# Elu from one exp and one max on products that carry a + 1, and the last layer's scores as extra columns of the eight-head layer

## The chip, the cores and the metric

The kernel runs on one core of one Trainium2 chip. The metric is the device time of one execution in microseconds (us). The engines are named as the profile does: PE (TensorE matmuls), PEld (TensorE weight loads), DVE (VectorE), ACT (ScalarE), POOL (GpSimd) and SP (SyncE, which issues most DMAs). Everything is fp32. Line numbers with an L are those of the kernel before, as its profile has them.

## The reference, cut to what matters

There are 128 independent graphs of 128 nodes with 512 features. Each passes four layers, and after each layer the input is added back and the sum is normalized over its features (`x = norm(x + layer(x))`).

- Layer 0: attention over the neighbours, scores from two dot products with `x`, output `attn @ x`.
- Layer 1: two graph attention layers. `xl = x @ W1` is 4 heads of 256, each with its own scores; the output of the four heads plus `b1` goes through an elu; then one head of 512 with `W2` and `b2`:

```python
h = jax.nn.elu(gat_layer(x, mask, W1, att_src1, att_dst1, b1, concat=True))
h = gat_layer(h, mask, W2, att_src2, att_dst2, b2, concat=False)
```

- Layer 2: 8 heads of 64, each with two score vectors, outputs concatenated.
- Layer 3: scores from `x @ W_fc.T` times the two halves of `W_attn`, attention applied to `x` itself, then an elu:

```python
h = jnp.einsum('bni,oi->bno', graph_input, W_fc)
f1 = jnp.einsum('bno,o->bn', h, a1)
f2 = jnp.einsum('bno,o->bn', h, a2)
...
h_prime = jnp.einsum('bnm,bmi->bni', attn, graph_input)
return jax.nn.elu(h_prime)
```

## The kernel before, in words

**One graph is one tile.** The 128 nodes lie on the 128 partitions. `graph(g)` (L314) lists the operations of one graph, each with its engine, an assumed cost, its inputs and its outputs; nothing is emitted there.

**A planner sets the order of every engine.** `Pipeline.plan` (L71) places the operations of one graph on the five engines, modulo a period (`PERIOD`, 24.7 before), from the assumed costs, fixed latencies (`LATENCY`), a weight on the rest of the path (`URGENCY`, 0.6) and a random shift for each operation (`SEED`, `SPREAD`: 62, 8.0). `Pipeline.run` (L124) then lays 128 copies of that plan one period apart, sorts all operations by planned time and emits them in that order. So many graphs are in flight at once, each engine runs its instructions strictly in that order, and the real times follow from the waits alone. A buffer gets a slot by its planned life; there are 8 PSUM banks. The loads and preparations of the weights are further entries with planned times of their own (`at(t, ...)`, L206).

**What one graph does:**

- Layer 0: two scores of `x` on VectorE (`score`, L493: multiply, add up, L495), `spread` (L326: transpose of a score column on VectorE, a DMA to a row in DRAM, a DMA that broadcasts it over the partitions), `attend` (L378), `mixed` (L467: one 512-column product of the attention with `x`), `resid` (L512), `norm` (L419).
- `attend` for some heads: leaky relu on ScalarE (L387), mask and row minimum on VectorE (L395), exp with its row sum on ScalarE (L404), reciprocal (L412), and with `scaled=True` a multiplication by the reciprocal on GpSimd (L414). Without it, the reader of the product multiplies. Then `turned` (L343): the attention is transposed by 32x32 blocks on VectorE (L348), written to DRAM and read back by DMA.
- `norm`: statistics on VectorE (L422, L423), the root on GpSimd (L426, L427), and the normalization on VectorE (L439), or with `on_act=True` on ScalarE (L435) with an offset from GpSimd (L432). After layer 2 it is on VectorE.
- Layer 1: `project` (L444) multiplies the transposed input with the weights in pieces of columns and copies each piece out of PSUM. `w1a` is 4 blocks of rows by 1032 columns (the 1024 of `W1` and 8 score columns), in 3 pieces of 344, evicted by ScalarE (L461). `block` (L535) makes half of the four heads' output in one bank, features on the partitions: 4 of the kernel's matmuls of 128 columns, 8 for both halves (L540). Then ScalarE makes exp(x + b1) and relu(x + b1), with `b1` as a bias for each partition, so in four pieces of 128 columns each (L549), and VectorE makes min(exp - 1, relu), the elu (L555). `w2a` is 8 blocks by 514 columns in 2 pieces of 257.
- Layer 2: `wha` is 4 blocks by 528 columns (512 and 16 score columns) in 2 pieces of 264. `heads` (L579) does 4 heads: 4 products of 64 columns (L585) and a multiplication by the reciprocals on VectorE (L590). GpSimd adds the input (L598).
- Layer 3: two scores of the normalized `x3` on VectorE (L603, L604, with the columns `wf`), attention, a `mixed` product, exp and relu on ScalarE with the reciprocal as scale (L609, L610), min(exp - 1, relu) on VectorE (L611), the input added on GpSimd (L614), norm on ScalarE, output.

**A matmul of the kernel is two MATMUL records and two LDWEIGHTS records in the profile**, so the counts of the profile are twice those of the code.

**Preparation**, mixed into the first graphs: the loads of `w1a`, `w2a`, `b2t` and of the score vectors go over GpSimd's queue, those of `wha` over SP's, that of `b1t` over ScalarE's. VectorE makes the score columns of the weights: `dot` (L263) for `w1a` (32 times) and `w2a` (16 times), `dots` (L280) for `wha` (8 pairs of a multiplication and a reduction). `columns` (L294) makes `wf` with two products (L298).

Of the kernel before, what the change touches and what calls it, by code (L numbers as in the profile page):

```python
# [16 lines left out]
P = 128  # L17
# [10 lines left out]
PERIOD = 24.7  # L28
LATENCY = {"PE": (0.0, 0.8), "DVE": (0.15, 1.4), "ACT": (0.1, 1.4), "POOL": (0.1, 1.4), "SP": (6.0, 6.0)}
URGENCY = 0.6  # L30
BANKS = 8

SEED, SPREAD = 62, 8.0
# [117 lines left out]
def tile_gat_stack(  # L151
# [48 lines left out]
    nc.vector.memset(neghalf, -0.5)  # L200

# [18 lines left out]
    def passing(t, until, n, src=None):  # L220
# [8 lines left out]
    C1, C2, C3 = HF + 2 * H1, F + 2, F + 2 * H2  # L229
# [5 lines left out]
    w1a = weights(-19, [P, KF, C1], "w1a", *(  # L235
        (lambda w, b=b: w[b::4, :, :HF], w1.rearrange("(k b a) c -> b a k c", b=4, a=32)[b])
        for b in range(4)
    ))
    a1 = [passing(-18, 90, HF, a.rearrange(flat).partition_broadcast(P)) for a in (a1_src, a1_dst)]
    b1t = weights(-18, [P, KH], "b1t", (lambda w: w, b1.rearrange("(k p) -> p k", p=P)), by=nc.scalar)  # L240
    b2t = rows(16, b2, F, "b2t")
    w2a = weights(18, [P, KH, C2], "w2a", *(
        (lambda w, k=k: w[:, k : k + 2, :F], w2[k * P : (k + 2) * P].rearrange("(k p) c -> p k c", p=P))
        for k in range(0, KH, 2)
# [3 lines left out]
    fc = passing(60, 270, F, w_fc)  # L248
# [5 lines left out]
        (lambda w, b=b, k=k: w[b::4, k, :F].rearrange("p (h o) -> p h o", h=H2),  # L254
# [3 lines left out]
    acb = [passing(240, 270, P) for _ in range(2)]  # L258
    wf = const.tile([P, 2, F], F32, name="wf")
    prod = [passing(-20, 230, F) for _ in range(2)]  # L260
    turn = [0]
# [9 lines left out]
    for k in range(KF):  # L271
        for s in range(2):
            for h in range(H1):
                c, o = slice(h * FH, (h + 1) * FH), HF + s * H1 + h
                at((31, 33, 56, 58)[k] + s + h / 4, lambda k=k, s=s, c=c, o=o: dot(w1a[:, k, c], a1[s].ap[:, c], w1a[:, k, o : o + 1]))
    for k in range(KH):
        for s in range(2):
            at(100 + 3 * k + 1.5 * s, lambda k=k, s=s: dot(w2a[:, k, :F], a2[s].ap, w2a[:, k, F + s : F + s + 1]))

    def dots(k, s):  # L280

        turn[0] ^= 1
        pr = prod[turn[0]].ap
        nc.vector.tensor_mul(pr, wha[:, k, :F], a3[s].ap)
        nc.vector.tensor_reduce(
            out=wha[:, k, F + s * H2 : F + (s + 1) * H2], in_=pr.rearrange("p (h o) -> p h o", h=H2),
            op=ALU.add, axis=AX.X,
        )

    for k in range(KF):  # L290
        for s in range(2):
            at(190 + 6 * k + 3 * s, lambda k=k, s=s: dots(k, s))

    def columns(s):  # L294
# [4 lines left out]
        nc.vector.tensor_copy(wf[:, s, :], pf)  # L299

    for s in range(2):
        at(250 + 3 * s, lambda s=s: columns(s))
# [11 lines left out]
    def graph(g):  # L314
# [63 lines left out]
        def attend(db, h0, nh, src, mask, scaled=False):  # L378
# [34 lines left out]
            if scaled:  # L413
                op("POOL", 1.3, lambda: nc.gpsimd.tensor_mul(  # L414
# [4 lines left out]
        def norm(y, on_act=False):  # L419
# [10 lines left out]
            if on_act:  # L430
                mr = small("mr", 1)
                op("POOL", 0.3, lambda: nc.gpsimd.tensor_scalar(  # L432
                    out=mr.ap, in0=mv.ap[:, 0:1], scalar1=rd.ap, scalar2=-1.0, op0=ALU.mult, op1=ALU.mult
                ), [mv, rd], [mr])
# [3 lines left out]
                return  # L438
# [5 lines left out]
        def project(xT, wa, nk, ncol, nchunk, t, evict):  # L444

            w = ncol // nchunk

            def chunk(c, ev):
                px = bank()
                cols = slice(c * w, (c + 1) * w)  # L450

                for k in range(nk):
                    op("PE", w * 4 / 2400 + 0.006, lambda k=k: nc.tensor.matmul(  # L453
                        px.ap[:, :w], lhsT=xT.ap[:, k, :], rhs=wa[:, k, cols],
                        start=(k == 0), stop=(k == nk - 1),
                    ), [xT] if k == 0 else [xT, px], [px])
                if ev == "DVE":
                    op("DVE", 0.11 + w / 960, lambda: nc.vector.tensor_copy(  # L458
                        t.ap[:, cols], px.ap[:, :w]), [px], [t])
# [196 lines left out]
```

## Time and profile before

| | before |
|---|---|
| median of 3 runs | 3200.89 us (3199.28 to 3202.06) |
| the profiled execution | 3201.2 us |
| its span, first to last instruction | 3199.3 us |
| mean granted TensorE clock | 0.983 |
| PE busy | 3073.7 us (96%), 14212 records |
| DVE busy | 3003.9 us (94%) |
| ACT busy | 2444.6 us (76%) |
| POOL busy | 1563.7 us (49%) |
| DMA queue 1 | 589.44 MB, 74.8% of 16 engines' span |

Busy time is the time in which at least one record of the engine runs. Matmuls overlap in the records, so what one costs is read from the distance of starts, not from its duration. A group of the profile is named by line, engine, operation and tiles; most work tiles share the name `w`. The profile's window "10 graphs in mid-run" is 1000 to 1236.45 us, ten times the distance at which the same work of the next graph starts; in it DVE is busy 233.48 us, ACT 190.53 and POOL 121.27.

### The profile page before, as it was taken

The numbers are of one execution on the slowest core, as the hardware profiler recorded it, in microseconds if no ns is written. First come the engines' busy times: TensorE is split into PE (matmuls) and PEld (weight loads), VectorE is DVE, ScalarE is ACT, GpSimd is POOL, SyncE is SP. The second block draws the span as 40 slices with busy tenths as digits, with TensorE's granted clock in tenths as the row PEclk, the third lists the DMA queues.
The fourth block names the chain that finished last, engine by engine and source line by source line (L and its number), as shares of the span: only waits on it lengthen the run. The fifth ranks groups of instructions, "written<-read, shape, count | busy, mean of one in ns | idle before, by whom it ended". The sixth has DMA issues, their size and how long they took to land.

```text
span 3199.3 us, 60449 instructions
## 1 busy us (share of the span) xinstructions
PE 3073.7 (96%) x14212; PEld 2378.0 (74%) x14212; DVE 3003.9 (94%) x9976; ACT 2444.6 (76%) x8961; POOL 1563.7 (49%) x2328
## 2 busy tenths in 40 slices
PE   3999999999999999999999999999999999999974
PEld 1677777777777777777777777777777777777762
DVE  5768999999999999999999999999999999999885
ACT  1567888877878788788787887878878878788864
POOL 4334545555545455555455554545555545555334
PEclk9999999999999999999999999999999999999985
DMA  4467787777878777788787777777777787778774
GB/s 149 116 154 186 190 196 196 195 197 193 199 192 198 193 198 194 196 197 197 191 199 196 193 196 195 197 196 196 194 199 193 195 196 197 197 192 196 175 167 112
DMA packets 1640373, 600.46 MB, mean 188 GB/s; under 512 B 1310464, under 2 KB 1490688, under 8 KB 1640016
## 3 DMA queue, kind: packets, MB, share of 16 engines
q1 hardware_dynamic: 1636608, 589.44, 74.8%
q0 software_dynamic: 1936, 6.62, 0.6%
q8 instruction: 115, 1.88, 0.3%
q14 instruction: 242, 1.98, 0.2%
q10 hardware_dynamic: 1472, 0.53, 0.1%
HBM read 368.91 MB, written 227.48 MB: 186 GB/s over the span
## 4 chain that ended last, share of the span: by engine, by line
PE 93%; DVE 3%; DMA 2%; POOL 1%; ACT 1%; issue 1%; SPq 0%; ACTq 0%; POOLq 0%; DVEq 0%
PE ps L453 69%; PE ps L470 10%; PE ps L540 7%; PE ps L585 6%; DMA w<-scr 1%; DVE w L495 0%; PE ps L506 0%; DMA scr<-w 0%; ACT w L404 0%; DVE w L395 0%; DVE st L422 0%; DMA w_-1_4_139<-in_L_gnn_att_dst_dram 0%; POOL rd L427 0%; DVE w L348 0%; DVE w_-1_1_94 L266 0%
## 5 line engine op out<-in xcount | busy, mean ns | idle before, releaser
L453 PE MATMUL ps<-w2a,w 128*128 128x257 f32 x4096 | 953.2, 380 | 3.1 <-DVE xl L458 3.1
L453 PE MATMUL ps<-w1a,w 128*128 128x344 f32 x3072 | 917.2, 455 | 1.9 <-ACT w L549 0.9
L453 PEld LDWEIGHTS ps<-w2a,w 128*128 128x128 f32 x4096 | 758.3, 190 | 121.1 <-DVE xl L458 3.9
L453 PEld LDWEIGHTS ps<-w1a,w 128*128 128x128 f32 x3072 | 587.4, 191 | 348.6 <-issue 41.1
L404 ACT ACTIVATE w<-w,nm 128x128 f32<-128x128 f32 x1920 | 767.3, 412 | 31.9 <-DVE nm L395 26.6
L387 ACT ACTIVATE w<-w,xl 128x128 f32<-128x128 f32 x1664 | 543.5, 447 | 265.5 <-DVE w L513 239.6
L395 DVE CUSTOM_DVE_ANT_0 w<-w,w 128x128 f32<-128x128 f32 x1920 | 666.3, 456 | 24.7 <-ACT w L387 11.6
L549 ACT ACTIVATE w<-ps,b1t 128x128 f32<-128x128 f32 x2048 | 560.6, 404 | 112.3 <-PE ps L540 112.3
L348 DVE STREAM_TRANSPOSE w<-w 128x512 f32<-128x512 f32 (+1 forms) x1024 | 544.0, 541 | 32.3 <-PE ps L540 9.1
L426 POOL TENSOR_SCALAR rd<-mv 128x1 f32<-128x1 f32 x512 | 118.5, 232 | 920.5 <-DVE mv L423 894.3
L453 PEld LDWEIGHTS ps<-wha,w 128*128 128x128 f32 x2048 | 390.4, 191 | 121.4 <-issue 36.8
L453 PE MATMUL ps<-wha,w 128*128 128x264 f32 x2048 | 480.0, 388 | 0.0
L461 ACT COPY xl<-ps 128x344 f32<-128x344 f32 (+2 forms) x640 | 277.9, 435 | 175.3 <-PE ps L453 165.8
L404 ACT ACTIVATION_READ_ACCUMULATOR w<-w,nm 128x1 f32 x1920 | 401.2, 209 | 0.0
L523 POOL TENSOR_TENSOR w<-w,b2t 128x512 f32<-128x512 f32 x128 | 165.9, 1296 | 467.5 <-DVE w L348 282.0
L585 PEld LDWEIGHTS ps<-xl,w 128*128 128x128 f32 x2048 | 295.3, 197 | 104.2 <-issue 78.9
L422 DVE BATCH_NORM_STATS2 st<-w 128x6 f32<-128x512 f32 x512 | 353.9, 691 | 11.8 <-POOL w L614 7.3
L427 POOL TENSOR_TENSOR rd<-rd,neghalf 128x1 f32<-128x1 f32 x512 | 307.4, 600 | 42.7
L470 PE MATMUL ps<-w,w 128*128 128x512 f32 x512 | 281.7, 633 | 32.5 <-DMA w<-scr 16.1
L585 PE MATMUL ps<-xl,w 128*128 128x64 f32 x2048 | 278.5, 271 | 25.4 <-DVE mv L423 9.9
L395 DVE DVE_READ_ACCUMULATOR2_ANT nm<- 128x1 f32 x1920 | 291.4, 152 | 0.0
L495 DVE CUSTOM_DVE_ANT_0 w<-w,wf 128x512 f32<-128x512 f32 x256 | 282.2, 1103 | 0.0
(74 smaller groups left out, 3913.7 us busy)
## 6 DMA issues: line engine op xcount, KB each, us to landing
scr<-w SPq DMA_DIRECT2D x640, 256.0 KB
w<-scr SPq DMA_DIRECT2D x640, 256.0 KB
w<-row SPq DMA_DIRECT2D x128, 512.0 KB
w<-in_x_dram SPq DMA_DIRECT2D x128, 256.0 KB
w<-row SPq DMA_DIRECT2D x128, 256.0 KB
out_dram<-w SPq DMA_DIRECT2D x128, 256.0 KB
w<-row SPq DMA_DIRECT2D x384, 64.0 KB
scr<-w SPq DMA_DIRECT2D x384, 64.0 KB
```

The costliest lines, as they stand in the source:

```text
L348: op("DVE", 0.12 + 0.133 * n, lambda: nc.vector.transpose(zb.ap.rearrange("p b h c -> p h b c"), src.ap.rearrange("p (h b c) -> p h b c", ...
L387: nc.scalar.activation(z.ap[:, h, :], db.ap[:, h0 + h, :], AF.Prelu, bias=src(h0 + h), alpha=SLOPE)
L395: nc.vector.tensor_tensor_reduce(out=zz.ap[:, h, :].rearrange("p (b a) -> p a b", b=4), in0=z.ap[:, h, :].rearrange("p (a b) -> p a b", b= ...
L404: nc.scalar.activation(zz.ap[:, h, :], zz.ap[:, h, :], AF.Exp, bias=nm.ap[:, h : h + 1], scale=-1.0, accum_out=rs.ap[:, h : h + 1],)
L422: op("DVE", 0.6, lambda: nc.vector.bn_stats(st.ap, y.ap), [y], [st])
L427: nc.gpsimd.tensor_tensor(out=rd.ap, in0=rd.ap, in1=neghalf, op=ALU.pow)
L453: op("PE", w * 4 / 2400 + 0.006, lambda k=k: nc.tensor.matmul(px.ap[:, :w], lhsT=xT.ap[:, k, :], rhs=wa[:, k, cols], start=(k == 0), stop= ...
L461: op("ACT", 0.16 + w / 1200, lambda: nc.scalar.copy(t.ap[:, cols], px.ap[:, :w]), [px], [t])
L470: op("PE", width * 4 / 2400, lambda: nc.tensor.matmul(pa.ap[:, :width], lhsT=pt.ap[:, 0, :], rhs=xv.ap[:, :width], start=True, stop=True), ...
L495: op("DVE", 0.75, lambda: nc.vector.tensor_tensor_reduce(out=jk.ap, in0=xv.ap, in1=wv, scale=1.0, scalar=init, op0=ALU.mult, op1=ALU.add, ...
L549: nc.scalar.activation(out.ap[:, k, :], pa.ap[:, u * P : (u + 1) * P], func, bias=b1t[:, k : k + 1])
L585: op("PE", 0.225, lambda u=u, h=h: nc.tensor.matmul(pa.ap[:, u * FO : (u + 1) * FO], lhsT=pt.ap[:, u, :], rhs=xl3.ap[:, h * FO : (h + 1) * ...
```

## The change

- **Elu.** Since elu(v) + 1 = max(v + 1, min(exp(v), 1)), the products now carry v + 1: ScalarE makes exp(p - 1) of the product p in one instruction of 512 columns, VectorE makes max(min(exp, 1), p) with p read from PSUM. So Relu falls away in both Elus. In layer 1, `b1 + 1` is added to `xl` by GpSimd (two additions of 512 columns) after the scores were taken; since the attention is now scaled to sum 1, that adds it to the products. The + 1 that remains in the hidden features is taken out by preparation: minus the column sums of `w2a` go into `b2t` (`ones_out`) and into two score shifts (`shifts`), which one small addition of VectorE puts on each graph's scores (`sc2`). In layer 3, `norm` adds the 1 to its offset, the normalization moves from VectorE to ScalarE, and the attention is scaled by GpSimd (`scaled=True`).
- **Scores of the last layer.** They are linear in the normalized sum of layer 2's output and its input. So each head of `wha` gets two more columns (its rows times `wf`, by head), 66 columns for each head, and two columns for the input's own part; `wha` is 546 columns in 2 pieces of 273. The head products give the two partial scores beside the 64 features, VectorE adds up the 8 heads (16 elements), adds the input's part, and applies mean and root (`normed`). Both `score` calls after layer 2 fall away.
- **Pieces.** `w1a` is stored by head, 258 columns each (256 and 2 scores), in 4 pieces instead of 3. `w2a` is two halves of 256 with one score column each.
- **Loads.** `w1a` comes in 16 loads (4 before), `w2a` in 8 (4 before), `b1` as a row for all partitions over GpSimd's queue.
- **Planner.** `PERIOD` 24.9, `URGENCY` 1.0, `SEED` 17, `SPREAD` 3.0, some assumed costs; so the whole order is drawn anew.

```diff
-PERIOD = 24.7
+PERIOD = 24.9
-URGENCY = 0.6
+URGENCY = 1.0
-SEED, SPREAD = 62, 8.0
+SEED, SPREAD = 17, 3.0
...
+    def ones_out(s):
+        pf = psum.tile([P, 512], F32, tag=f"ps{6 + s}", name=f"pc_{s}")
+        for k in range(KH):
+            nc.tensor.matmul(
+                pf[:, : F // 2], lhsT=minus, rhs=w2a[:, k, s, : F // 2], start=(k == 0), stop=(k == KH - 1)
+            )
+        cols = slice(s * F // 2, (s + 1) * F // 2)
+        nc.vector.tensor_add(b2t[:, cols], b2t[:, cols], pf[:, : F // 2])
...
+    def shifts():
+        pf = psum.tile([P, 512], F32, tag="ps7", name="pc_2")
+        for k in range(KH):
+            nc.tensor.matmul(pf[:, :2], lhsT=minus, rhs=w2a[:, k, :, F // 2], start=(k == 0), stop=(k == KH - 1))
+        nc.vector.tensor_copy(shift2, pf[:, :2])
...
     for k in range(KF):
         for s in range(2):
-            at(190 + 6 * k + 3 * s, lambda k=k, s=s: dots(k, s))
+            at(160 + 12 * k + 6 * s, lambda k=k, s=s: dots(k, a3[s], slice(SH + s * H2, SH + (s + 1) * H2)))
+            at(163 + 12 * k + 6 * s, lambda k=k, s=s: dots(k, wf[s], slice(FO + s, SH, CH)))
...
+        for k in range(KF):
+            pf = psum.tile([P, 512], F32, tag="ps7", name=f"pg_{k}")
+            nc.tensor.matmul(pf[:, :2], lhsT=fcp.ap[:OUT, k * P : (k + 1) * P], rhs=ac, start=True, stop=True)
+            nc.vector.tensor_copy(wha[:, k, C3 - 2 :], pf[:, :2])
...
+        for h in range(0, H1, 2):
+            op("POOL", 1.3, lambda h=h: nc.gpsimd.tensor_add(
+                xl.ap[:, h : h + 2, :FH], xl.ap[:, h : h + 2, :FH],
+                b1t[:, h * FH : (h + 2) * FH].rearrange("p (h c) -> p h c", h=2),
+            ), [xl], [xl])
...
-            op("ACT", 1.1, lambda: biased(e1, AF.Exp), [pa], [e1])
-            op("ACT", 1.1, lambda: biased(r1, AF.Relu), [pa], [r1])
-            op("DVE", 0.6, lambda: nc.vector.scalar_tensor_tensor(
-                out=half(hT), in0=half(e1), scalar=-1.0, in1=half(r1), op0=ALU.add, op1=ALU.min
-            ), [e1, r1], [hT])
+            op("ACT", 0.6, lambda: nc.scalar.activation(half(e1), pa.ap, AF.Exp, bias=minus[:, 0:1]), [pa], [e1])
+            op("DVE", 0.65, lambda: nc.vector.scalar_tensor_tensor(
+                out=half(hT), in0=half(e1), scalar=1.0, in1=pa.ap, op0=ALU.min, op1=ALU.max
+            ), [e1, pa], [hT])
...
-        norm(x3)
-        score(x3, wf[:, 1, :], 0.0, sc4, 1)
-        score(x3, wf[:, 0, :], 0.0, sc4, 0)
+        def scores():
+            nc.vector.tensor_reduce(
+                out=sc4.ap, in_=z3.ap[:, :, FO:].rearrange("p h s -> p s h"), op=ALU.add, axis=AX.X
+            )
+            nc.vector.tensor_add(sc4.ap, sc4.ap, xl3.ap[:, C3 - 2 :])
+
+        op("DVE", 0.2, scores, [z3, xl3], [sc4])
+        mv, rd = norm(x3, on_act=True, plus=1.0)
+
+        def normed():
+            nc.vector.scalar_tensor_tensor(
+                out=sc4.ap, in0=swf, scalar=mv.ap[:, 0:1], in1=sc4.ap, op0=ALU.mult, op1=ALU.add
+            )
+            nc.vector.tensor_scalar_mul(sc4.ap, sc4.ap, rd.ap)
+
+        op("DVE", 0.15, normed, [sc4, mv, rd], [sc4])
...
-        op("ACT", 0.7, lambda: nc.scalar.activation(e3.ap, pa.ap, AF.Exp, scale=ri.ap), [pa, ri], [e3])
-        op("ACT", 0.7, lambda: nc.scalar.activation(r3.ap, pa.ap, AF.Relu, scale=ri.ap), [pa, ri], [r3])
-        op("DVE", 0.6, lambda: nc.vector.scalar_tensor_tensor(
-            out=y.ap, in0=e3.ap, scalar=-1.0, in1=r3.ap, op0=ALU.add, op1=ALU.min
-        ), [e3, r3], [y])
+        op("ACT", 0.6, lambda: nc.scalar.activation(e3.ap, pa.ap, AF.Exp, bias=minus[:, 0:1]), [pa], [e3])
+        op("DVE", 0.65, lambda: nc.vector.scalar_tensor_tensor(
+            out=y.ap, in0=e3.ap, scalar=1.0, in1=pa.ap, op0=ALU.min, op1=ALU.max
+        ), [e3, pa], [y])
```

## The prediction, as put on record

> **What bounds the kernel now.** I read the page's busy shares and its chain first, then TensorE's timeline over one graph in mid-run, then stretches of the span, and last the groups of VectorE, ScalarE and GpSimd. The page's shares of busy time and of the chain that ended last:
>
> ```profile
> PE 3073.7 (96%) x14212; PEld 2378.0 (74%) x14212; DVE 3003.9 (94%) x9976; ACT 2444.6 (76%) x8961; POOL 1563.7 (49%) x2328
> ...
> PE 93%; DVE 3%; DMA 2%; POOL 1%; ACT 1%; issue 1%; SPq 0%; ACTq 0%; POOLq 0%; DVEq 0%
> ```
>
> TensorE carries 93% of the chain, but VectorE is nearly as busy, so busy shares alone don't settle it. The timeline of TensorE does (start, us, then the group; "idle before" would stand in brackets):
>
> ```profile
> 999.77 6.81 PE L453 MATMUL ps<-w1a,w 128*128 128x344 f32 x23
> 1006.43 3.20 PE L453 MATMUL ps<-w2a,w 128*128 128x257 f32 x14
> 1009.46 0.33 PE L585 MATMUL ps<-xl,w 128*128 128x64 f32 x2
> ...
> 1016.51 1.45 PE L585 MATMUL ps<-xl,w 128*128 128x64 f32 x12
> 1017.80 1.08 PE L470 MATMUL ps<-w,w 128*128 128x512 f32 x2
> 1018.71 3.72 PE L453 MATMUL ps<-wha,w 128*128 128x264 f32 x16
> 1022.27 1.02 PE L470 MATMUL ps<-w,w 128*128 128x512 f32 x2
> ```
>
> No line has an idle time: each group starts where the last ends. Start to start, a 344-column matmul record costs 6.66/23 = 289 ns, a 257-column one 3.03/14 = 217 ns, a 264-column one 3.56/16 = 222.5 ns: a slope of (289 - 222.5)/80 = 0.83 ns a column and about 2.5 ns besides. The 64-column ones cost 1.29/12 = 107 ns, far over what that slope gives; they are held by their weight loads. One graph costs 23.65 us, as the chain shows too:
>
> ```profile
> 384.87 9.97 PE ps L453 x38
> 408.52 9.97 PE ps L453 x38
> ```
>
> The stretches of the span (us, busy PE, PEld, DVE, ACT, POOL with counts, then granted clock, DMA share, GB/s):
>
> ```profile
> 0.00:100.00 100.00, 41.46 (x106) 22.65 (x107) 55.37 (x202) 19.74 (x66) 39.34 (x62) 0.92 0.52 147
> 100.00:225.00 125.00, 120.89 (x518) 89.36 (x518) 83.71 (x264) 72.81 (x268) 40.88 (x61) 0.99 0.49 126
> 225.00:3040.00 2815.00, 2815.00 (x13238) 2197.97 (x13237) 2753.75 (x9130) 2261.03 (x8327) 1419.24 (x2107) 1.00 0.79 195
> 3040.00:3187.00 147.00, 94.50 (x354) 67.79 (x353) 108.60 (x378) 87.28 (x296) 58.66 (x89) 0.72 0.62 146
> ```
>
> From 225 to 3040 us TensorE is busy for every microsecond. So span = 128 x 23.65 = 3027 us of matmuls, and 172 us of fill and drain. Summing over all matmuls the time to the next start beyond its full-clock spacing splits the 172 into 12 us before the first matmul, 67 up to 225 us, 80 from 3040 us to the last matmul, 11.5 after it, and some 2 of setup products.
>
> The groups that the change touches (name, shapes, count, then busy us, mean ns, idle before):
>
> ```profile
> L495 DVE CUSTOM_DVE_ANT_0 w<-w,wf 128x512 f32<-128x512 f32 x256 | 282.2, 1103 | 0.0
> ...
> L439 DVE TENSOR_SCALAR w<-w,mv,rd 128x512 f32<-128x512 f32 x256 | 243.2, 950 | 4.6 <-POOL rd L427 3.9 <-issue 0.6
> ...
> L523 POOL TENSOR_TENSOR w<-w,b2t 128x512 f32<-128x512 f32 x128 | 165.9, 1296 | 467.5 <-DVE w L348 282.0 <-PE ps L453 153.8 <-DMA w<-row 21.6
> ...
> L611 DVE SCALAR_TENSOR_TENSOR w<-w,w 128x512 f32<-128x512 f32 x128 | 153.5, 1199 | 0.4 <-ACT w L609 0.4
> ...
> L609 ACT ACTIVATE w<-ps,ri 128x512 f32<-128x512 f32 x128 | 85.6, 668 | 1.1 <-DVE sc L495 1.1
> ```
>
> **What the Trainium skill says.** "TensorE: Matmul & The Clock Gate", section "Back-to-back issue gap", gives columns/2.4 + 2.5 ns for a warm matmul; the trace agrees with twice the column term for each fp32 record (344 x 2/2.4 + 2.5 = 289.2). The same page, "LDWEIGHTS (loading the stationary operand)", gives columns/1.2, 107 ns for 128: that is the 107 ns of the 64-column products, so their width is free. "GPSIMD Engine Reference", "Specifications": its SBUF interfaces are shared with VectorE, against operations with two SBUF inputs or in a two-port mode. The trace agrees for L495 with wf, 676 ns in mid-run where no GpSimd work overlaps, against a mean of 1116 there, but not everywhere: L555, also with two SBUF inputs, takes 675 either way.
>
> **The change, part by part, per graph in mid-run.**
> TensorE. First layer: 24 records of 344 columns (24 x 289.2 = 6.940) become 32 of 258 (32 x 217.7 = 6.966): +0.03. Second layer: 257 columns as before: 0. Third layer: 16 of 264 become 16 of 273, 222.5 + 9 x 0.83 = 230.0: +0.12. Head products 64 to 66 columns: 0, hidden under the weight load (uncovered, 16 x 1.7 = 0.03). The rest is unchanged. Sum +0.148 us, so 23.79 us a graph, and 128 x 0.148 = +18.9 us, all on the path.
>
> VectorE. Off: two scores L495 (2 x 1.12, 2 x 0.08 for their read-outs), one of two L439 (1.01), the last Elu reading PSUM and no longer two SBUF tiles (1.28 to the 0.72 of L513): -3.97. On: the first Elu from PSUM, 2 x 0.05; a 16-element reduce, three tiny operations and the sum of second-layer scores, 5 x about 0.13 (L412's 119 ns to L423's 179): +0.75. So 23.35 (ten graphs in mid-run, 233.5 us busy) falls by 3.2 to about 20.1, before more GpSimd overlap. Overlap now adds about 3.7 us (each group's mean less its mean clear of GpSimd), of which some 1.7 stays exposed; with GpSimd busier by a third that grows by 0.6. 20.7 is under 23.79: nothing on the path.
>
> ScalarE, 19.05: 16 biased activations, union 4.38, become 2 of 512 columns at 0.67 (-3.05); one Relu off (-0.67); third norm on (+0.81); one more eviction (+0.1 to +0.5). About 16.4: hidden. GpSimd, 12.1: b1 adds 2 x 1.29, the last layer's scaling 0.36 (between L414's 1.04 for four heads and 0.23), mr and its +1, 0.53 + 0.23: about 15.8. The b1 adds follow the evictions; in the new order a graph's mixing products come two graphs after its first layer's, so some 45 us hide them. If POOL were late, they would hold those products and w2a behind them. SP's issues stay equal in number.
>
> Fill. (a) w1a takes 16 loads for 4 on GpSimd's queue, at about 0.55 us each, w2a 8 for 4, b1t moves there with 512 KB more: +10 us of issue ahead of graph 0's and 1's masks. Most is hidden: GpSimd idles 4.9 and 7.7 us there. But 16 products of minus and w2a (32 records, 7 to 14 us by clock) now stand before graph 0's first mixing product at 33.5 us, and the b1t add waits on its load at VectorE. I take +3 (0 to +9). (b) The shift products and last columns: 24 records x 0.112 = 2.7, and four round trips with VectorE at about 0.5: +4.7 (2 to 7). (c) In the new order w2a of the first three or four graphs follows directly on that graph's mixing products; in the old one 9 w2a products, a mixing product and w1a lie between. So TensorE waits for exp, Elu and release, about 2 us a graph: +7 (2 to 10), until later layers fill the gap. The 16 dot pairs of 1.37 us (8 before) double to 22 us of VectorE in the same rounds, and take part of that cover; no more added. Sum about +14.
>
> Drain. In the new order a final mixing product comes 3 graphs behind its heads, not 4, so one product fewer follows the last heads; the last graph's path loses a norm and two scores (about 2.5), a Relu (0.67), and gains POOL's scaling and two tiny steps (0.9). With VectorE lighter in the thinned rounds: -7 (0 to -16).
>
> Against the profiled execution (3201.2, span 3199.3): 3201.2 + 18.9 + 14 - 7 = 3227; the runs' median is 0.3 lower, 3200.9. I predict 3227.
>
> **The rivals.** *The drain repays it (not slower).* In the drained rounds TensorE waits for loads of transposed attention, behind VectorE's queue:
>
> ```profile
> 3080.00:3100.00 20.00, 13.16 (x44) 9.62 (x43) 16.05 (x56) 12.17 (x43) 8.58 (x13) 0.66 0.72 179
> 3100.00:3120.00 20.00, 13.32 (x44) 9.37 (x43) 12.62 (x48) 11.72 (x39) 6.26 (x11) 0.74 0.67 149
> ```
>
> VectorE is busy 65 to 80% there, so if its queue sets each round, nine rounds x 2.9 us = 26 us come off; with a fill of only +5: 3201.2 + 18.9 + 5 - 26 = 3199. It decides once drain gains exceed fill costs by about 13 us. Against it: the waits named are DMA landings, which no edit shortens. *A new wait in mid-run.* VectorE against a busier GpSimd refills, or w2a waits for the Elu each graph: 0.3 us x 120 = 36, so 3263. For it: VectorE is at 99% now and several of its operations stretch. Against: it would have to regain 3 us, and 7 us of other products lie between mixing products and w2a in mid-run. *The widths cost nothing*: the added columns would be absorbed only if TensorE had waits now to fill (3227 - 18.9 = 3208); the stretch from 225 to 3040 shows none.
>
> **How the numbers follow.** A measurement of this kernel tells about 0.2%, 6.4 us, from no change. Forecast (TensorE-bound, fill loses, drain gains a little): 0.75, all but about 0.01 of it slower. Drain repays: 0.15, of it 0.06 faster, 0.08 same, 0.01 slower. New wait: 0.09, slower. Free widths: 0.01, about the same or slower. So faster 0.06, same 0.10, slower 0.84. Range: the low end takes the fill at +3 and the drain at -16 with widths as priced, 3207, and reaches to 3205; the high end the fill at +26 and no drain gain, 3246, and reaches a little into the new wait: 3250. Left out: about 0.12 below, 0.07 above.
>
> **What would show it.** Right: a mid-run period of 23.79 us with no idle on TensorE; 258-column records at 217.7 ns and 273-column ones at 230; VectorE near 20.7 us a graph; more lost before 225 us, with waits of w2a for the first Elu and of the setup products; the last heads and the end closer by a few us. Wrong: a period other than 23.79; 66-column products above 112 ns; idle of TensorE in mid-run; or fill and drain whose sum falls by more than 12 us.

## The result and the profile after

The kernel after takes 3254.94 us (median of 4 runs, 3254.07 to 3255.78) against 3201.07 for the kernel before in the same session: ratio 1.0169, 95% interval 1.0151 to 1.0187, 54 us slower. The forecast was 3227 with a range of 3205 to 3250. Slower was right, and so was what bounds the kernel; the size was half of what came, and outside the range.

The profiled execution has a span of 3253.7 us and a mean granted clock of 0.977. Its busy shares and the shares of its chain:

```profile
PE 3113.7 (96%) x15292; PEld 2582.4 (79%) x15292; DVE 2862.7 (88%) x10005; ACT 2143.7 (66%) x7297; POOL 1906.0 (59%) x2985
...
PE 93%; DVE 3%; DMA 2%; issue 1%; POOL 1%; ACT 0%; SPq 0%; POOLq 0%; DVEq 0%; ACTq 0%
```

VectorE and ScalarE are lighter and GpSimd is heavier, as announced, and the chain is TensorE's as before. The groups that took the place of those shown for before (columns as there):

```profile
L626 DVE SCALAR_TENSOR_TENSOR w<-w,ps 128x512 f32<-128x512 f32 x256 | 165.3, 646 | 5.3 <-PE ps L515 4.9 <-ACT w L625 0.4
L585 POOL TENSOR_TENSOR w<-w,b2t 128x512 f32<-128x512 f32 x128 | 164.5, 1285 | 214.5 <-ACT xl L522 179.2 <-PE ps L515 19.0 <-DVE w L504 13.6
...
L699 ACT ACTIVATE w<-ps,minus 128x512 f32<-128x512 f32 x128 | 86.3, 674 | 6.3 <-PE ps L530 6.2
```

VectorE's part of the Elu costs 646 ns where 0.72 us was priced, ScalarE's 674 ns where 0.67 was. The scores L603 and L604 and the Relus have no counterpart. None of it is on the path in mid-run: in ten graphs there (1000 to 1238.45 us) VectorE is busy 219.9 us, ScalarE 167.1 and GpSimd 147.2, so 22.0, 16.7 and 14.7 a graph, against 20.7, 16.4 and 15.8 forecast.

Stretches of the span (us, busy PE, PEld, DVE, ACT, POOL, then clock, DMA share, GB/s):

```profile
0.00:100.00 100.00, 45.41 (x162) 33.60 (x163) 54.72 (x193) 13.95 (x44) 50.97 (x78) 0.86 0.50 142
100.00:225.00 125.00, 108.60 (x460) 86.36 (x459) 84.51 (x227) 39.94 (x133) 48.40 (x59) 0.88 0.37 95
225.00:3040.00 2815.00, 2815.00 (x14048) 2351.93 (x14048) 2581.10 (x9056) 1968.52 (x6723) 1718.76 (x2685) 1.00 0.79 193
```

TensorE again has no idle from 225 to 3040 us. The second line has changed most: from 100 to 225 us TensorE is busy 108.6 us instead of 120.9, at a clock of 0.88 instead of 0.99. One graph of TensorE in mid-run:

```profile
1001.96 1.03 PE L515 MATMUL ps<-w2a,w 128*128 128x257 f32 x4
1002.83 1.95 PE L619 MATMUL ps<-w,xl 128*128 128x128 f32 x16
...
1005.91 1.45 PE L659 MATMUL ps<-xl,w 128*128 128x66 f32 x12
1007.20 1.07 PE L530 MATMUL ps<-w,w 128*128 128x512 f32 x2
...
1011.90 0.56 PE L659 MATMUL ps<-xl,w 128*128 128x66 f32 x4
1012.29 5.86 PE L515 MATMUL ps<-w2a,w 128*128 128x257 f32 x26
```

The drain, in the stretches that stand as far behind the last first-layer product (3075.0 us for 3015.0) as those shown of before:

```profile
3140.00:3160.00 20.00, 12.19 (x38) 8.65 (x39) 13.71 (x58) 14.02 (x53) 6.25 (x14) 0.74 0.66 159
3160.00:3180.00 20.00, 13.62 (x49) 9.65 (x47) 12.28 (x45) 10.07 (x36) 7.33 (x14) 0.66 0.52 128
```

VectorE has 13.7 and 12.3 us of work there for 16.1 and 12.6, and TensorE is no busier for it (12.2 and 13.6 us for 13.2 and 13.3). The distance from graph to graph in mid-run is 23.843 us (first-layer products of the 21st and 111th graph), where 23.79 was forecast.

**Where the 54 us are.** The run has three parts: the fill (here up to 250 us), in which the first graphs enter and few others can fill a wait; mid-run; and the drain (from 3040 us), in which the last graphs leave. For each kernel I add up the matmul records at their full-clock spacing (columns x 2/2.4 + 2.5 ns, 109 ns where the weight load is longer) and, by stretch, the time to the next start beyond that, idle or slow ("lost"; the drain with what follows the last matmul). The sums meet the spans within 0.7 us.

| profile of | median of runs | span | matmul work | lost to 250 us | 250 to 3040 | from 3040 |
|---|---|---|---|---|---|---|
| before | 3201.1 | 3199.3 | 3023.6 | 79.8 | 4.7 | 91.8 |
| after | 3254.9 | 3253.7 | 3051.0 | 99.4 | 11.2 | 92.5 |
| no_columns | 3246.0 | 3241.0 | 3048.4 | 86.9 | 11.1 | 94.9 |
| no_ones | 3246.7 | 3245.6 | 3042.4 | 100.7 | 11.2 | 91.8 |
| no_prep | 3242.5 | 3240.2 | 3039.8 | 94.8 | 11.1 | 95.0 |
| own_bank | 3244.8 | 3241.1 | 3051.0 | 89.8 | 11.2 | 89.7 |
| after_redraw | 3245.8 | 3244.6 | 3051.0 | 94.6 | 10.7 | 88.7 |
| elu_apart | 3224.5 | 3223.2 | 3051.0 | 80.6 | 5.3 | 86.7 |
| apart_no_prep | 3208.8 | 3207.9 | 3039.8 | 79.2 | 5.3 | 84.0 |
| drain_load | 3238.4 | 3236.3 | 3051.0 | 83.9 | 5.1 | 96.6 |
| before_new_order | 3198.6 | 3200.7 | 3023.6 | 83.4 | 6.6 | 87.5 |
| before_no_scores | 3192.5 | 3188.0 | 3023.6 | 75.8 | 4.6 | 84.3 |

So after against before: work +27.4 (widths 17.9, new setup products 9.5), fill +19.6, mid-run +6.5, drain +0.7. The widths were forecast at 18.9. The fill with its setup products, forecast at +14, came to 29.1; mid-run beyond the widths, forecast at 0, to 6.5; the drain, forecast at -7, to 0.7. Each row is one profile, and these scatter: the fill and the drain of two kernels that are alike there differ by 3 to 6 us (`split_scores`, which changes only the last 10 graphs of before, loses 75.1 in the fill for 79.8).

**What the fill waits for.** TensorE while the second and third graph pass (the bracket is the idle before, and what ended it):

```profile
131.17 1.95 PE L619 MATMUL ps<-w,xl 128*128 128x128 f32 x16
132.95 0.60 PE L515 MATMUL ps<-w2a,w 128*128 128x257 f32 x2
134.47 0.33 PE L568 MATMUL ps<-ident,w 128*128 128x128 f32 x1 [0.92 <-POOL w L546]
137.42 8.53 PE L515 MATMUL ps<-w2a,w 128*128 128x257 f32 x26 [2.63 <-DVE w L569]
...
154.47 1.95 PE L619 MATMUL ps<-w,xl 128*128 128x128 f32 x16
156.26 0.60 PE L515 MATMUL ps<-w2a,w 128*128 128x257 f32 x2
158.96 0.33 PE L568 MATMUL ps<-ident,w 128*128 128x128 f32 x1 [2.10 <-POOL w L546]
162.32 8.03 PE L515 MATMUL ps<-w2a,w 128*128 128x257 f32 x26 [3.03 <-DVE w L569]
```

L619 is the mixing products (`block`); the 26 records of w2a that follow belong to the same graph. Three things stand between. The transposed mask of a later graph (L568) waits for GpSimd's mask. Then w2a waits, and not only for its Elu: the named releaser is L569, VectorE's product with that transposed mask. And then the same 26 records take 8.53 and 8.03 us, where mid-run has 5.86. VectorE in front of the first of them:

```profile
134.02 0.65 DVE L626 SCALAR_TENSOR_TENSOR w<-w,ps 128x512 f32<-128x512 f32 x1
134.59 0.96 DVE L637 TENSOR_TENSOR sc<-xl,shift 128x2 f32<-128x2 f32 x1
...
135.72 0.73 DVE L330 TENSOR_TENSOR w_-1_2_98<-wha,w_-1_5_303 128x512 f32<-128x512 f32 x1
136.49 0.69 DVE L334 TENSOR_REDUCE wha<-w_-1_2_98 128x8 f32<-128x512 f32 x1
137.09 0.28 DVE L569 TENSOR_TENSOR w<-ps,noneye 128x128 f32<-128x128 f32 x1
```

The Elu (L626) ends at 134.67. L569 is queued behind the small shift addition and one of the setup pairs (L330, L334), ends at 137.37, and w2a starts at 137.42. For these graphs the planner put the transposed mask and the first products of w2a into one PSUM bank. In before, the same place has other work. There the second graph's mixing products (L540) are followed by w2a of the graph before it, a mixed product and the next graph's w1a, and its own w2a comes at 124.94:

```profile
110.56 1.95 PE L540 MATMUL ps<-w,xl 128*128 128x128 f32 x16
112.34 1.03 PE L453 MATMUL ps<-w2a,w 128*128 128x257 f32 x4
...
113.32 3.20 PE L453 MATMUL ps<-w2a,w 128*128 128x257 f32 x14
117.04 1.13 PE L470 MATMUL ps<-w,w 128*128 128x512 f32 x2 [0.52 <-DVE xl L458]
118.00 7.10 PE L453 MATMUL ps<-w1a,w 128*128 128x344 f32 x24
124.94 3.20 PE L453 MATMUL ps<-w2a,w 128*128 128x257 f32 x14
```

The clock in after, in the same columns as the stretches above:

```profile
137.40:142.00 4.60, 4.58 (x11) 3.65 (x12) 4.50 (x8) 0.00 (x0) 0.00 (x0) 0.50 0.84 173
142.00:146.00 4.00, 4.00 (x18) 3.42 (x17) 1.80 (x3) 1.28 (x4) 0.00 (x0) 0.90 0.66 187
```

After the wait the clock is 0.50, and the starts of the first dozen records lie 427 to 431 ns apart (the first two 591), then 217. So the wait costs 2.67 us more than its own length (8.53 for 5.86). This is the gate of the Trainium skill's "TensorE: Matmul & The Clock Gate", section "What's actually happening": half the clock after an idle window of about 3.4 us, back after about as long of busy time. The trace agrees in kind; here idle times of 0.92 and 2.63 us, broken by one short product, were enough, and the slow part lasted about 5 us.

### The profile page after: what moved, and what is told of

The parts are those of the page before. It is cut to its first block, busy times and chain, and to the rows that moved or that the text cites. A ratio compares the mean times of both kernels' runs of the same rounds, so it can differ in the third digit from the quotient of the medians.

```text
span 3253.7 us, 61851 instructions
## 1 busy us (share of the span) xinstructions
PE 3113.7 (96%) x15292; PEld 2582.4 (79%) x15292; DVE 2862.7 (88%) x10005; ACT 2143.7 (66%) x7297; POOL 1906.0 (59%) x2985
## 4 chain that ended last, share of the span: by engine, by line
PE 93%; DVE 3%; DMA 2%; issue 1%; POOL 1%; ACT 0%; SPq 0%; POOLq 0%; DVEq 0%; ACTq 0%
PE ps L515 69%; PE ps L530 10%; PE ps L619 7%; PE ps L659 6%; DVE w L454 1%; DMA w<-row 1%; DMA w<-scr 0%; PE ps L568 0%; DVE w L407 0%; DVE st L481 0%; PE pc L297 0%; DMA w2a<-in_L_gnn_W_dram 0%; DMA w1a<-in_L_gnn_W_dram 0%; DVE w L700 0%; DVE w L557 0%
## 5 line engine op out<-in xcount | busy, mean ns | idle before, releaser
L515 PE MATMUL ps<-w1a,w 128*128 128x258 f32 x4096 | 917.6, 382 | 0.3 <-DMA w<-scr 0.3
L515 PEld LDWEIGHTS ps<-w1a,w 128*128 128x128 f32 x4096 | 779.1, 190 | 173.2 <-issue 59.5
L454 DVE CUSTOM_DVE_ANT_0 w<-w,w 128x128 f32<-128x128 f32 x1920 | 852.2, 563 | 14.2 <-ACT w L446 13.9
L522 ACT COPY xl<-ps 128x258 f32<-128x258 f32 (+2 forms) x768 | 289.7, 377 | 409.1 <-PE ps L515 393.8
L446 ACT ACTIVATE w<-w,xl 128x128 f32<-128x128 f32 x1536 | 474.2, 391 | 88.4 <-DMA w<-row 68.5
L515 PE MATMUL ps<-wha,w 128*128 128x273 f32 x2048 | 511.1, 396 | 13.9 <-DMA w<-scr 13.9
L500 ACT ACTIVATE w<-w,mr,rd 128x512 f32<-128x512 f32 x384 | 309.0, 807 | 89.3 <-POOL mr L493 81.4
L704 POOL TENSOR_TENSOR w<-w,w 128x512 f32<-128x512 f32 x128 | 163.0, 1274 | 316.6 <-DVE w L700 316.6
L603 POOL TENSOR_TENSOR xl<-xl,b1t 128x512 f32<-128x512 f32 x256 | 312.6, 1241 | 0.0
L671 POOL TENSOR_TENSOR w<-z,w 128x512 f32<-128x512 f32 x128 | 151.4, 1183 | 243.6 <-PE ps L515 135.8
```

The source lines that it names most:

```text
L446: nc.scalar.activation(z.ap[:, h, :], db.ap[:, h0 + h, :], AF.Prelu, bias=src(h0 + h), alpha=SLOPE)
L454: nc.vector.tensor_tensor_reduce(out=zz.ap[:, h, :].rearrange("p (b a) -> p a b", b=4), in0=z.ap[:, h, :].rearrange("p (a b) -> p a b", b= ...
L500: op("ACT", 0.6, lambda: nc.scalar.activation(y.ap, y.ap, AF.Identity, bias=mr.ap, scale=rd.ap), [y, rd, mr], [y])
L522: op("ACT", 0.06 + w / 1200, lambda: nc.scalar.copy(dst(), px.ap[:, :w]), [px], [t])
L603: op("POOL", 1.3, lambda h=h: nc.gpsimd.tensor_add(xl.ap[:, h : h + 2, :FH], xl.ap[:, h : h + 2, :FH], b1t[:, h * FH : (h + 2) * FH].rearr ...
```

## The experiments

My theory on the result was: the order and the setup cost the fill some 29 us, the widths and something small in the order cost 25 in mid-run, and the drain gains nothing. Rivals: the preparation alone makes the fill; the drain is set by VectorE and was repaid; the widths are free. Ratios are against the kernel before on the same chip.

**The preparation.** `no_columns`: the calls of `columns`, `last_columns` and half of the `dots` fall away.

```diff
-        at(142 + 3 * s, lambda s=s: columns(s))
-    at(150, last_columns)
+    at(150, no_columns)
...
-            at(163 + 12 * k + 6 * s, lambda k=k, s=s: dots(k, wf[s], slice(FO + s, SH, CH)))
```

> The kernel after, without the preparation of the last layer's score columns: the two products that spread the last weights, the four small products, and 8 of the 16 multiply-and-reduce pairs of VectorE are left out and the columns set to zero (so the last layer's scores are wrong); the order of the graphs and every width stay as after, 3255. Theory 'order': in the first four graphs TensorE stands behind exp and Elu because w2a follows directly, and VectorE's pairs only lengthen that: the waits of 3 us shrink to about 2, four times, and some 3 us of small products go: 3247 (3243 to 3251). Rival 'preparation': the pairs are what holds the Elu, so halving them gives back half or more of the 26 us lost between 100 and 200 us: 3235 to 3242. Rival 'nothing': the pairs lie beside other waits: 3252 to 3255.

Measured: 3246.04, ratio 1.0146 (1.0131 to 1.0162), 8.9 us less than after. `no_ones` drops `ones_out` and `shifts`.

> The kernel after, without the column sums of w2a (16 products ahead of the first mixing product, and the 8 small ones for the score shifts; the shifts are set to zero and b2t is left as loaded, so scores and layer 2's input are wrong). The products are 9.7 us of TensorE at 28 us, in a time in which it waits for the first attention, whose own start was 4.3 us later than before. Theory 'order': the products fill a wait; the first mixing product comes about 4 us earlier and the small products save 1: 3250 (3247 to 3254). Rival: the setup products stand on the path in full, 9.6 us of records: 3243 to 3246. Rival: nothing comes of it, since the loads set the first attention: 3254 to 3256.

Measured: 3246.66, ratio 1.0145 (1.0130 to 1.0160), 8.3 less, more than I expected. The first w1a starts at 49.6 us for 54.5: that is 5 of it. `no_prep` drops both.

> The kernel after without both preparations: no score columns of the last layer (set to zero) and no column sums of w2a (shifts zero), so scores and layer 2's input are wrong; the order of the graphs as after. Alone they gave 3246.0 and 3246.7. Theory: they cost in different stretches (before 54 us; 100 to 200 us), so they add: 3238 (3234 to 3241), and what still stands above the kernel before is 25 in mid-run and 12 in the fill. Rival: the first only shifts the second, and together they give little more than one, 3243 to 3246.

Measured: 3242.47, ratio 1.0128 (1.0113 to 1.0143), 12.5 less: the two don't add up to 17, the rival is nearer. And 41 us of the 54 stay without either preparation, so it isn't the main cause.

**The widths.** `wide`: 18 columns of zeros more in `wha`, and nothing else.

```diff
+    CW = C3 + 18
...
-    wha = weights(70, [P, KF, C3], "wha", *(
+    wha = weights(70, [P, KF, CW], "wha", *(
```

> The kernel after, with 18 columns of zeros more in wha (two pieces of 282 for 273; the planner is told the old costs, so the order is the same). Theory 'TensorE is full': 16 records x 9 columns x 0.83 ns = 0.12 us a graph, x 128 = +15.3: 3270 (3268 to 3273), mid-run period 23.97. Rival 'widths cost nothing' (some other wait sets the period and would take the columns up): 3254 to 3258.

Measured: 3267.62, ratio 1.0218 (1.0201 to 1.0235), 12.7 more; the distance of graphs is 23.963 us for 23.843, exactly the 0.12. The median is 2.7 short of 15.4; the profile, which lost 5.5 us less in the fill than that of after, shows how much the fill varies. In mid-run, widths are paid in full.

**VectorE and the drain, from the side of before.** `before_no_scores`:

```diff
-        score(x3, wf[:, 1, :], 0.0, sc4, 1)
-        score(x3, wf[:, 0, :], 0.0, sc4, 0)
+        blank(x3, sc4, 1)
+        blank(x3, sc4, 0)
```

> The kernel before, with the last layer's two scores replaced by a write of zero to each score (so the last layer's attention is wrong); the order of all work is unchanged. It takes 2 x 1.2 us of VectorE off each graph, and off the last graph's path. Theory: in mid-run and in the drain TensorE waits for landings and not for VectorE's load, so the time falls by no more than the last graph's own 2.4 us: 3198 to 3201, with the mid-run period at 23.65. Rival 'VectorE sets the drain' (the one by which the change would have repaid itself): nine rounds by about 2 us: 3180 to 3188.

Measured: 3192.45, ratio 0.9975 (0.9967 to 0.9984), 8.4 less. That lies between the two forecasts. The profile, which is of a faster run than the median, shows 7.5 of it in the drain and 4.0 in the fill. So the relief that the change aims at exists, and at both ends of the run, not in mid-run (period 23.645 in both).

**The order.** In after, the planner may use the new Elu so early that w2a comes straight behind the mixing products. `elu_apart` tells it that the Elu is usable 2 us later:

```diff
-SEED, SPREAD = 17, 3.0
+SEED, SPREAD = 11, 3.0
...
-            ), [e1, pa], [hT])
+            ), [e1, pa], [hT], 2.0)
```

> The kernel after, with the planner told that the first Elu is usable 2 us later than it assumes (and seed 11, for a plan that fits). In its order the next graph's first-layer products and 4 of w2a of the graph before (11.4 us of early work) lie between a graph's mixing products and its w2a; in the order of after 0.5 us of such work lies there. Nothing else is changed. Theory 'order': what is left of the fill's loss after the two preparations, about 12 us, is w2a standing directly behind exp and Elu: the lost time between 100 and 200 us falls from 33 to 20 or less, and the total to 3243 (3238 to 3248), if the drain stays. Rival 'preparation alone' (the waits are VectorE's pairs, and they hold whatever comes next): 3252 to 3258.

Measured: 3224.52 (3222.60 to 3228.84), ratio 1.0075 (1.0060 to 1.0090): 30.4 us less than after, more than the theory asked. The lost time between 100 and 200 us falls from 33.0 to 16.1 us. By the table, 18.8 of the 30 lie in the fill, 5.9 in mid-run and 5.8 in the drain, so the edit does more than set w2a apart. In the same place as above, its TensorE now does:

```profile
120.79 1.95 PE L619 MATMUL ps<-w,xl 128*128 128x128 f32 x16
122.58 1.03 PE L515 MATMUL ps<-w2a,w 128*128 128x257 f32 x4
123.45 0.27 PE L568 MATMUL ps<-ident,w 128*128 128x128 f32 x1
123.56 2.77 PE L515 MATMUL ps<-w2a,w 128*128 128x257 f32 x12
126.35 1.12 PE L530 MATMUL ps<-w,w 128*128 128x512 f32 x2
127.31 0.60 PE L515 MATMUL ps<-w1a,w 128*128 128x258 f32 x2
129.24 6.76 PE L515 MATMUL ps<-w1a,w 128*128 128x258 f32 x30 [1.32 <-DVE w L626]
135.84 3.63 PE L515 MATMUL ps<-w2a,w 128*128 128x257 f32 x16
```

Behind the mixing products come the rest of the former graph's w2a and the whole w1a of the next, 13 us before this graph's own w2a (135.84), and from 120 to 200 us no stop of w2a is left. Other products still stop there, at most for 2.75 us (1.32 here), and the clock stays full after it. The mid-run period falls to 23.792. Here is one graph of it:

```profile
1002.73 0.33 PE L659 MATMUL ps<-xl,w 128*128 128x66 f32 x2
1002.89 2.00 PE L619 MATMUL ps<-w,xl 128*128 128x128 f32 x16
...
1005.60 0.33 PE L659 MATMUL ps<-xl,w 128*128 128x66 f32 x2
1005.77 0.28 PE L568 MATMUL ps<-ident,w 128*128 128x128 f32 x1
...
1009.35 1.45 PE L659 MATMUL ps<-xl,w 128*128 128x66 f32 x12
1010.63 1.08 PE L530 MATMUL ps<-w,w 128*128 128x512 f32 x2
```

A pair of 66-column records alone takes 0.16 us (1002.73 to 1002.89), not 2 x 0.107: the first, behind a wide product, lasts 57 ns; I read that as its weight load being hidden behind the wide one. The record after the head products lasts about 54 ns longer (271 for 217 of w2a, 483 for 429 of 512 columns), except the mask's transposition (L568). This order enters the head products three times and pays for leaving them twice; the order of after (12 and 4 records) two and two. That is the 0.05 us.

`before_new_order` gives the kernel before the constants of after (24.9, 1.0, seed 4, spread 3.0), which puts its stages as far apart as those of `elu_apart`; `after_redraw` is after with seed 7.

> The kernel before, drawn with the planner's constants of after (24.9, 1.0, spread 3.0, seed 4, since 17 doesn't fit): every product and width as before, the same distances in graphs between the stages as in 'elu_apart'. Theory: no fill loss comes of it, since early work lies between mixing products and w2a in it too, and a redrawn order is worth a few us by itself; the mid-run period keeps 23.65: 3201 (3192 to 3208). Rival 'the new constants are what costs': 3215 or more. Read beside 'elu_apart', the difference is the change without the change of order: the widths and the preparation, 19 to 25 in mid-run and 17 in the fill, so some 40.

> The kernel after with seed 7 for 17: a control for what a redrawn order does where w2a still follows directly on the mixing products. Theory 'order': the fill loses as in after, 3255 (3248 to 3262). If any redraw moved the time as much as 'elu_apart' does, that kernel would show nothing about the place of w2a.

Measured: 3198.55, ratio 0.9997 (0.9989 to 1.0006), no change; and 3245.77, ratio 1.0134 (1.0117 to 1.0151), 9 less than after, a little below what I gave it. `after_redraw` keeps the stops of w2a (2.63, 3.03 and 2.07 us). So a redraw can move the time by 9 us, and the constants by themselves cost nothing; the two draws with w2a straight behind the Elu lie 21 and 30 us above `elu_apart`, 14 and 19 of it in the fill. Only one draw with w2a set apart was run.

**Elu or bank?** `own_bank` is after with the transposed mask in a PSUM bank that no other product of the first nine graphs uses (from the tenth graph on, one other product uses it; some products move to other banks by this edit too):

```diff
+                    if getattr(b, "own", False):
+                        b.slot, b.ap = 7, None
+                        b.ap = self.place(b, g)
+                        continue
...
         pm = bank()
+        pm.own = True
```

> The kernel after (3254.9) with the transposed mask in a PSUM bank that no other product of the graphs uses. In after, w2a of the second to fourth graph starts at 137.4, 162.3 and 185.8 us, each within 0.1 us of the end of the mask's product at L569, while its Elu is done at 134.7 and 159.9. Theory 'the bank is half of it': w2a then starts at the Elu, 2.5 us earlier each time, three times, and a little from the half clock: 3245 (3240 to 3249). Rival 'the Elu alone': the bank's wait ends together with another that stays (the transposition itself stands ahead of w2a and waits for GpSimd's mask): 3252 to 3256.

Measured: 3244.84, ratio 1.0144 (1.0127 to 1.0160), 10.1 less. (Lines are 4 or 5 further down.)

```profile
132.83 0.33 PE L573 MATMUL ps<-ident,w 128*128 128x128 f32 x1 [0.91 <-POOL w L550]
133.18 3.71 PE L519 MATMUL ps<-w2a,w 128*128 128x257 f32 x16
138.29 2.44 PE L519 MATMUL ps<-w2a,w 128*128 128x257 f32 x10 [1.40 <-DVE w L631]
...
154.21 0.33 PE L573 MATMUL ps<-ident,w 128*128 128x128 f32 x1 [2.58 <-POOL w L550]
155.26 7.30 PE L519 MATMUL ps<-w2a,w 128*128 128x257 f32 x26 [0.72 <-DVE w L631]
```

The wait of 2.63 us is gone, 1.40 for the second half's Elu comes in its place; GpSimd's mask stays. So a third of the order's 30 us goes with a bank that w2a shared with a step that has nothing to do with it.

**The rest of the preparation.** `apart_no_prep` is `elu_apart` with the edits of `no_prep`.

> 'elu_apart' (3224.5) without both preparations (no columns of the last layer, no column sums of w2a; both set to zero, so scores and layer 2's input are wrong). Above 'before_new_order' (3198.6) 'elu_apart' has 26 us, of which the widths are 128 x 0.147 = 18.8. Theory: the rest is the preparation, so about 7 us come off and the widths stay: 3217 (3214 to 3220). Rival 'in this order the preparation lies in waits': 3222 to 3225, and the 7 us are something else, such as GpSimd's additions of b1.

Measured: 3208.77, ratio 1.0026 (1.0016 to 1.0035): 15.8 less, not 7. Of the 26 us that `elu_apart` stands above `before_new_order`, 18.8 are widths (128 x 0.147) and 15.8 preparation. The remainder is -8.6. About 1.7 of it (an estimate: 4 records of 429 ns) are the two L340 products, which `before_new_order` has too; -6.9 is left over, and I read it as relief, though nothing measured it as such.

**What eats the relief in the drain?** `no_b1` leaves out GpSimd's two additions; `drain_load` puts two multiply-and-reduce instructions into `normed` in the last 10 graphs.

> 'elu_apart' without GpSimd's additions of b1 (b1 is left out of the first layer; the planner still plans them, so the order is the same). 2.6 us of GpSimd go from each graph, ahead of its mixing products. Theory (the prediction's): other work lies beside them, nothing on the path: 3222 to 3226. Rival 'GpSimd's longer chain holds the mixing products in the fill and the drain': one stretch of 2.6 us in three or four thinned rounds at either end, 3210 to 3218.

> 'elu_apart' with two multiply-and-reduce instructions of 512 columns put back on VectorE ahead of the last layer's score arithmetic (results unused), in the last 10 graphs alone: the load and the place that the two scores had. In the kernel before, their removal gave 8.4 us, 7.4 of it in the drain, and yet the drain of 'elu_apart' loses as much as that of 'before_new_order' (86.7 and 87.5 us). Theory A, 'the relief is there, and something else of the change eats it': the load costs what it gave, +5 to +9: 3230 to 3234. Theory B, 'landings and order set this drain, VectorE doesn't': only the last graph's own 2.4 us or less: 3224 to 3227.

Measured: 3222.64, ratio 1.0069 (1.0056 to 1.0081), 1.9 less, within the scatter: the additions are hidden. They aren't without effect: in ten graphs of mid-run (1000 to 1237.92 us) VectorE is busy 205.2 us without them and 223.0 with them, while the period is 23.792 us in both. And 3238.44, ratio 1.0117 (1.0103 to 1.0131), 13.9 more, 9.9 of it in the drain (the fill, which this edit doesn't touch, differs by 3.3): theory A, and stronger. Three more kernels looked for what takes the relief away, each in the last 10 graphs only: `norm_vector` (third norm by VectorE), `scale_vector` (last attention scaled by VectorE), and, on the kernel before, `split_scores` (one score by GpSimd and ScalarE).

> 'elu_apart' (3224.5) with the third norm back on VectorE in the last 10 graphs, in one instruction and without the + 1 (so these graphs' output is wrong), and GpSimd's offset and + 1 left out there. Theory 'GpSimd's steps eat the relief': the offset, the + 1, a hop and ScalarE's 0.81 us stand in each last-layer chain for VectorE's 1.0: 3 to 6 us come back, 3219 to 3222. Rival 'not this': VectorE's load grows by 1 us a graph, which by 'drain_load' (2.4 us a graph for 10 to 14 us) costs 4 to 6: 3228 to 3231.

> 'elu_apart' with the last layer's attention scaled by VectorE instead of GpSimd in the last 10 graphs. Theory 'GpSimd's steps eat the relief': two hops between engines and 0.1 us go from each chain, 1 to 3 us come back: 3221.5 to 3223.5. Rival: no change, or a microsecond lost to VectorE's load: 3224 to 3226.

> The kernel before with the second of the last layer's two scores made by GpSimd (product) and ScalarE (sum) instead of VectorE, in the last 10 graphs alone; no width and no setup product changes. Leaving out both scores gave 8.4 us. Theory 'VectorE's queue sets the drain': half of the drain's 7.4 us comes off: 3197 (3195 to 3199), a version faster than both. Rival: the second score then arrives later through two more engines, and takes that back: 3200 to 3203.

Measured: 3225.48, ratio 1.0078 (1.0065 to 1.0092); 3226.86, ratio 1.0083 (1.0069 to 1.0096); 3205.52, ratio 1.0014 (1.0008 to 1.0021). The first two give nothing back (+1.0 and +2.3 against `elu_apart`). That doesn't clear GpSimd's steps, since each of the two also puts work on VectorE: `norm_vector` lies between its two forecasts, where a gain and a loss that cancel would put it. The third is 5.5 us slower than before, more than its rival allowed.

`last_elu_only` was the try at a version that beats both.

> A version that could beat both: 'before_new_order' with only the last layer's Elu from exp and max (the last norm carries + 1 and goes to ScalarE, its attention is scaled on GpSimd, the two scores start from minus the column sums). No width of TensorE changes and no setup product is added. Theory: the mid-run stays at 23.65, the drain gains some of the 1.6 us of VectorE and 0.7 of ScalarE in each graph: 3195 (3190 to 3200), against 3198.6. Rival: GpSimd's scaling, offset and + 1 lengthen the last layer's chain as much: 3199 to 3204.

Measured: 3200.84, ratio 1.0001 (0.9992 to 1.0009): the rival's range. This kernel has GpSimd's new steps without the widths and the setup, and VectorE's saving brings nothing. No version here that computes the whole reference beats the kernel before clear of the noise.

## Why the prediction was right or wrong

- **TensorE bounds, widths are paid: right.** 0.148 us a graph was the sum; with the stages in the same order, `elu_apart` against `before_new_order`, it is 23.792 - 23.645 = 0.147. Records of 258 and 273 columns took 217.5 and 230.3 ns, 66-column ones 105 on average.
- **"The rest is unchanged. Sum +0.148 us, so 23.79 us a graph": wrong by the neighbours.** The order of after adds 0.05, 6 us in all. I read the head products' mean (107 ns) as their price anywhere; it depends on what stands before and behind.
- **VectorE at 20.7 us a graph: too low, without effect on the time.** 22.0 came. I had 0.6 for the growing overlap with GpSimd; the additions of b1 alone take 1.8 us a graph of VectorE (22.3 to 20.5 by `no_b1`). My counterexample L555 isn't one: in mid-run of before, the only GpSimd work beside it is L432, of one element for each partition.
- **Fill (a), "I take +3 (0 to +9)": above the +3, within its range.** The products of `minus` delay the first w1a by 5 us; all of `no_ones` is 8.3 with the shift products. (The three terms of the fill add up to 14.7, not 14.)
- **Fill (b), "take part of that cover; no more added": failed.** I priced the columns' TensorE time and round trips and gave VectorE's doubled pairs nothing. `no_columns`, without both, is 8.9 less, against +4.7 for all of (b); its matmul records make up 2.6 of it. How the rest divides between pairs and round trips wasn't tried. (a) and (b) together, 7.7 by the sum, cost 15.8 in `elu_apart` (some 14 without L340).
- **Fill (c), "w2a ... follows directly on that graph's mixing products ... about 2 us a graph: +7 (2 to 10)": the step that missed most.** The place was right, the size wrong: `elu_apart` takes 18.8 us off the fill. A graph loses not 2 but about 6 us: 6.2 at 134 us (0.92 + 2.63 idle + 2.67 of slow clock), and the next two in the same way 7.3 and 5.1. I counted the Elu and left out three things: the mask from GpSimd and its transposition standing in between, the bank that they share with w2a behind VectorE's setup pairs (10 us by `own_bank`), and the half clock after each stop, though I had it in view for the setup products.
- **Drain, "a final mixing product comes 3 graphs behind its heads ... -7": the step came true, the sum didn't.** +0.7 came. In after four final products follow the last heads, in before five, and from the last heads to the end 27.5 us are lost for 32.2. But between the last w2a and the last `wha` product 37.1 are lost for 30.3. The last `wha` waits 9.82 us for a DMA in after and for nothing in `elu_apart`:

```profile
3187.52 5.58 PE L515 MATMUL ps<-wha,w 128*128 128x273 f32 x16 [9.82 <-DMA w<-scr]
...
3154.10 5.37 PE L515 MATMUL ps<-wha,w 128*128 128x273 f32 x16
```

The six kernels with after's order (after, `no_columns`, `no_ones`, `no_prep`, `own_bank`, `wide`) lose 35 to 40 us there and 90 to 95 in the whole drain. The five in `elu_apart`'s order without extra load (`elu_apart`, `apart_no_prep`, `no_b1`, `norm_vector`, `scale_vector`), which also have only four final products behind the last heads, lose 25 to 28 and 84 to 87. I looked only at the end of the new order, not at what comes ahead of it. What in that order makes `wha` late wasn't tried; it stays open.

- **"With VectorE lighter in the thinned rounds": shown for before, not for the change.** The scores alone are worth 8.4 us in the kernel before. But with the stages in the same order only 1 to 3.5 us of relief show in the drain (86.7 and 84.0 against 87.5, a profile of the slowest run of `before_new_order`). Why stays open; GpSimd's added steps are neither shown to be the reason nor ruled out.
- **"A new wait in mid-run" didn't come,** and the high end of the range, built from the fill at +26, had no room for +29 in the fill and +6 in mid-run together.

By edits: order +30.4, preparation beyond that of before about +14.1, widths +18.8, new constants for before -2.5 (which is not clear of noise). These make 60.8; the -6.9 that is missing to 53.9 is the remainder that I read as relief.

## What to carry to other kernels

When an order is redrawn, read the fill of the new order instruction by instruction for the first graphs: for each product, what precedes it on its engine, who fills its bank last, and what is queued ahead of that on the other engines. A shorter operation can make a planner put its reader right behind it, which brings no wait in a full pipeline (none from 225 to 3040 us here) and costs most where nothing else is there yet. And price a stop of TensorE of some 3 us at up to twice its length.

## What was not expected of the hardware

- A 66-column product in the first place behind a wide one costs 57 ns, further ones 109 to 112, and the first wide product behind them 54 ns more; L568 behind them doesn't pay that. My reading, which no run isolates: the weight load is moved, not saved.
- Idle times of 0.92 and 2.63 us with one 0.33 us product between were enough for the half clock (428 ns for 217), for about 5 us.
- GpSimd's two additions of 512 columns a graph lengthen VectorE's busy time by 1.8 us a graph, and not the period.
- The order of work alone moves this kernel by 30 us, more than the widths (18.8) or the preparation (15.8).
